# Attention gathers in a graph network: 16 nodes by 8 slots against 32 nodes by 4 slots, with a count of rounds for each group of 32 and new bounds of the kept counts

## The chip, the cores and the metric

The kernel runs on one core of one Trainium2 chip. The metric is the device time of one execution in microseconds (us). A core has five engines, each with its own queue of instructions worked off in order: TensorE (PE) multiplies matrices, VectorE (DVE) and ScalarE (ACT) do elementwise work, GpSimd (POOL) does elementwise work and issues the indirect transfers (gathers and scatters by row index), SyncE (SP) issues plain transfers.

## The reference

Two layers over a graph of 4096 nodes with 128 features. `adj` is a symmetric random matrix with the diagonal set; a node has some 40 to 100 neighbours.

```python
# layer 0: graph attention, 8 heads
Wh = einsum('nd,hde->hne', nodes, W)
f1 = einsum('hnd,hd->hn', Wh, a1);  f2 = einsum('hnd,hd->hn', Wh, a2)
e = leaky_relu(f1[:, :, None] + f2[:, None, :], 0.2)
att = softmax(where(adj > 0, e, -9e15), axis=-1)
h = elu(einsum('hnm,hmd->hnd', att, Wh))
x = elu(concat_heads(h) @ W1 + b1)
x = layernorm(nodes + x) * gamma + beta
# layer 1: every (num_nbr / 2)-th neighbour of a node is dropped, the rest are kept
vals = where(keep[:, :, None], x[None], big)
svals = sort(vals, axis=1)                      # per node and per feature
agg = mean over q in (.25, .5, .75) of svals[ceil(q * n_keep) - 1]
out = (0.5 * agg + 0.5 * x) @ W.T + b + x
```

## The kernel before

The program goes through four stages.

**Lists.** `neighbours` reads `adj` and makes, for every node, the list of its neighbours' ids (up to `C1` = 104). `arrange` counts them, works out how many are kept, and sorts the nodes by that count: 32 tiles of 128 nodes, tile 0 with the smallest counts. Its result goes to `meta_d` in DRAM, one row of `MW` = 216 words for each node at its place in the order. A row is cut into `SL` parts of `PART` words; in each part the first `FULL` words hold every `SL`-th neighbour (padded with row 0 of the table, whose logit is a large negative number), the others hold the kept ids for layer 1 and the node's own id. `column(k)` says where the k-th of these other words stands.

**The choice of a branch.** The tables `LOW` and `HIGH` are the smallest and the largest kept count that tile t is taken to hold. `arrange` compares the graph's counts with them (`lower`, `upper`, lines 367 to 377 and 527) and raises a flag if one is broken. With the flag raised `general` runs, a path without these lists; otherwise `gat` and `sparse` do.

**`gat`, layer 0 on the lists.** For a tile of 128 nodes the lists are gathered so that one indirect transfer fills 128 partitions with `NJ` nodes times `SL` slots: before, 16 nodes by 8 slots. A tile is `GR` = 8 groups of 16 nodes, and a group takes `rounds[t]` transfers, the largest count of the tile plus 2 divided by 8 and rounded up, so that all groups of a tile take the same number. A transfer (line 637) brings for each partition a row of 136 numbers from `xf_d`: 128 features and 8 logits f2. `probabilities` copies the logits out (`f2`, ACT, line 661), turns them through DRAM (`e_d`) so that a partition is one node, does the softmax, and turns the result back (`p_d`, `pr`). `combine` builds for every group the tile `spread` (DVE, line 701): for each round, the probability of partition p at the columns of its node and zero at the columns of the other nodes, `NJ` * `H` = 128 columns. Then one float32 matmul a round (line 711), with the gathered rows as the stationary operand and `spread` as the moving one, adds into `ps_z`. Two products with `W` and `W1`, the layernorm and a scatter of the 128 finished rows to `x1_d` (line 758) follow. The loop issues the gathers of tile t + 1 ahead of the work on tile t. Gathered rows live in a pool of 18 buffers (`nb`), 8 of them a tile. The work on tile t + 1 is told to stand behind the last steps of tile t.

**`sparse`, layer 1.** For tile t all `HIGH[t]` rows of kept neighbours are gathered from `x1_d` (line 1185, one transfer for each place in the list, and one, `xs`, for the nodes' own rows). A network of comparators then sorts the places, elementwise over nodes and features: `compare` copies the low operand (ACT, line 1219), and takes minimum and maximum (DVE, lines 1220 and 1221), or only one of them where only one is needed (lines 1223 and 1225). `places(t)` gives, from `LOW[t]` and `HIGH[t]`, the ranks that a quartile can fall on; only comparators that these need are kept. Where `HIGH[t]` is over 64 and not over 80, the rows past 64 (`extra`) are sorted apart and brought in at the wanted ranks through the tile `cut` (lines 1235 to 1250). `finish` weighs the ranks that can be a quartile (one step at line 1265 or 1268 for each), and ends with a small product, two additions (`o`, lines 1280 and 1281) and a scatter (line 1282). Comparators of the second half of tile t - 1 and of the first half of tile t are interleaved on DVE. `rows` has 3 buffers, so the gathers of tile t + 1 wait for the last step at line 1268 of tile t - 2.

A scheduler puts each engine's instructions in an order when the kernel is built; steps of one tile can stand among those of another. The addition `o` = `xs` + bias (line 1280) of a tile stands early, soon after its gathers begin.

Of the kernel before, what the change touches and what calls it, by code (L numbers as in the profile page):

```python
# [38 lines left out]
F32 = mybir.dt.float32  # L39
F16 = mybir.dt.float16  # L40
BF = mybir.dt.bfloat16
I32 = mybir.dt.int32
# [3 lines left out]
ALU = mybir.AluOpType  # L46
# [4 lines left out]
P = 128  # L51
N = 4096
D = 128
NT = N // P
H = 8
NCH = N // 512
BIG = float(2**53)
# [15 lines left out]
CAND = C1 + C2 + C3 * PEELS  # L73
WBITS = 16
NG1 = N // WBITS
SL = 8
NJ = P // SL
GR = P // NJ
XF = D + 2 * H
FULL = C1 // SL  # L80
PART = FULL + 14
MW = SL * PART
NODE, POS = C1, C1 + 3
MIDDLE = 64
# [261 lines left out]
def arrange(tc, nc, c, lists, spill, negative, meta_d, flag_d):  # L346
# [5 lines left out]
    with tc.tile_pool(name="ar", bufs=1) as tp, tc.tile_pool(  # L352
        name="ar2", bufs=2
# [28 lines left out]
        for t in range(NT):  # L382
# [32 lines left out]
        own = tp.tile(classes, BF, name="own_c")  # L415
# [4 lines left out]
            op=ALU.is_equal,  # L420
# [4 lines left out]
        width = NT // 4 * NC  # L425
# [34 lines left out]
        for i in (1, 2):  # L460
            at = tp.tile([P, NT], F32, name="at", bufs=2)
# [13 lines left out]
        first = tp.tile([P, NT], F32, name="first")  # L475
# [104 lines left out]

def gat(tc, nc, c, xf_d, meta_d, w, w1, b1, gamma, beta, x1_d):

    rounds = [-(-(h + 2) // SL) for h in HIGH]
    most = max(rounds)
    with ExitStack() as ctx:
        one = ctx.enter_context(tc.tile_pool(name="ga1", bufs=1))
        tp = ctx.enter_context(tc.tile_pool(name="ga2", bufs=2))
        rowp = ctx.enter_context(tc.tile_pool(name="ga3", bufs=2 * GR + 2))
        dram = ctx.enter_context(tc.tile_pool(name="ga_d", bufs=2, space=DRAM))
        psum = ctx.enter_context(tc.tile_pool(name="ga_ps", bufs=2, space=PSUM))  # L590
        psum1 = ctx.enter_context(tc.tile_pool(name="ga_ps1", bufs=1, space=PSUM))
# [12 lines left out]
        ids = one.tile([P, GR * sum(rounds)], I32, name="ids")  # L604
        first = [GR * sum(rounds[:t]) for t in range(NT)]
        for t in range(NT):
            r = rounds[t]
            nc.sync.dma_start(
                out=ids[:, first[t] : first[t] + GR * r].rearrange("p (g r) -> p g r", g=GR),
                in_=dram_view(meta_d, t * P * MW, [[PART, P], [PART * P, GR], [1, r]]),  # L610
            )
# [8 lines left out]
        own, f1, den = small[:, :NJ], small[:, NJ : NJ + H], small[:, NJ + H :]  # L620
        nc.vector.reduce_sum(own, c["idf"].rearrange("p (j s) -> p j s", s=SL), axis=AX.X)

        def load(t):
            r = rounds[t]
            me = tp.tile([P, XF], F32, name="me", bufs=3)
            nc.gpsimd.indirect_dma_start(
                out=me,
                out_offset=None,
                in_=xf_d,
                in_offset=bass.IndirectOffsetOnAxis(ap=info[:, t, 1:2], axis=0),  # L630
            )
            groups = []
            for g in range(GR):
                rows = rowp.tile([P, most, D + H], F32, name="nb")
                for i in range(r):
                    at = first[t] + g * r + i
                    nc.gpsimd.indirect_dma_start(  # L637
                        out=rows[:, i, :],
                        out_offset=None,
                        in_=xf_d,  # L640
                        in_offset=bass.IndirectOffsetOnAxis(ap=ids[:, at : at + 1], axis=0),
                    )
                groups.append(rows)
            return me, groups

        def probabilities(t, me, groups):

            r = rounds[t]
            width = r * H
            e_d = dram.tile([P * SL * most * H], F32, name="e_d")  # L650
            p_d = dram.tile([P * SL * most * H], F32, name="p_d")

            def by_row(d):
                return dram_view(d, 0, [[width, P], [width * P, GR], [1, width]])

            def by_node(d):
                return dram_view(d, 0, [[width * SL, P], [1, width * SL]])

            f2 = tp.tile([P, GR, most * H], F32, name="f2")
            for g, rows in enumerate(groups):  # L660
                nc.scalar.copy(  # L661
                    f2[:, g, :width].rearrange("p (r h) -> p r h", h=H), rows[:, :r, D:]
                )
# [24 lines left out]
            nc.sync.dma_start(out=pr[:, :, :width], in_=by_row(p_d))  # L688
            return pr

        def combine(t, me, groups, pr):

            r = rounds[t]
            zT = tp.tile([P, H, P], F32, name="zT", bufs=1)
            for half in range(2):
                ps_z = psum.tile([P, GR // 2, NJ * H], F32, name="ps_z")
                for k in range(GR // 2):
                    g = half * (GR // 2) + k
                    spread = tp.tile([P, most, NJ, H], F32, name="spread")
                    shape = [P, r, NJ, H]  # L700
                    nc.vector.tensor_tensor(  # L701
                        spread[:, :r],
                        pr[:, g, : r * H]
                        .rearrange("p (r h) -> p r h", h=H)
                        .unsqueeze(2)
                        .to_broadcast(shape),
                        own.unsqueeze(1).unsqueeze(3).to_broadcast(shape),
                        op=ALU.mult,
                    )
                    for i in range(r):  # L710
                        nc.tensor.matmul(  # L711
                            ps_z[:, k, :],
                            groups[g][:, i, :D],
                            spread[:, i].rearrange("p j h -> p (j h)"),
                            start=i == 0,
                            stop=i == r - 1,
                        )
# [12 lines left out]
            for h in range(H):  # L730
# [991 lines left out]
```

## Time and profile before

| what | us |
|---|---|
| median of three runs | 9627.47 (9623.37 to 9630.22) |
| the profiled execution | 8855.54 |
| its span, first to last instruction | 8853.8 |
| lists and arrange, to the first gather of `gat` at | 872.77 |
| `gat`, from there to the start of its last scatter | 2998.89 |
| `sparse`, 3874 to 8843 | 4969 |

The profiled execution was 771.9 us shorter than the median of the runs; the profile shows nothing of that difference. Busy time of an engine is the time in which at least one of its instructions ran. An idle time in brackets is that of the engine just before the instruction, with what ended it; `issue` is time in which nothing that the profile shows was waited for.

Over the span the engines were busy: PE 890.4 us, DVE 6064.2 us, ACT 2178.9 us, POOL 4453.2 us.

### The profile page before, as it was taken

The numbers are of one execution on the slowest core, as the hardware profiler recorded it, in microseconds if no ns is written. First come the engines' busy times: TensorE is split into PE (matmuls) and PEld (weight loads), VectorE is DVE, ScalarE is ACT, GpSimd is POOL, SyncE is SP. The second block draws the span as 40 slices with busy tenths as digits, with TensorE's granted clock in tenths as the row PEclk, the third lists the DMA queues.
The fourth block names the chain that finished last, engine by engine and source line by source line (L and its number), as shares of the span: only waits on it lengthen the run. The fifth ranks groups of instructions, "written<-read, shape, count | busy, mean of one in ns | idle before, by whom it ended". The sixth has DMA issues, their size and how long they took to land. (4 is left out here: it accounts for less than half of the span.)

```text
span 8853.8 us, 31211 instructions
## 1 busy us (share of the span) xinstructions
PE 890.4 (10%) x6299; PEld 816.5 (9%) x6299; DVE 6064.2 (68%) x8106; ACT 2178.9 (25%) x2202; POOL 4453.2 (50%) x4633
## 2 busy tenths in 40 slices
PE   2110122122322322210000000000000000000000
PEld 1110122121222222210000000000000000000000
DVE  7996122222222222227989999999999988999999
ACT  2110011010100000003333333333333333333333
POOL 0002777777777777755444544545354543345510
PEclk5555566566666666655555555555555555555555
DMA  3221333333323332321111111111011110011100
GB/s 137 106 89 26 72 67 70 70 66 69 70 67 72 67 68 68 68 48 40 34 31 30 37 30 30 36 28 38 25 38 25 35 30 23 23 30 34 32 7 1
DMA packets 285892, 428.52 MB, mean 48 GB/s; under 512 B 179669, under 2 KB 196440, under 8 KB 277496
## 3 DMA queue, kind: packets, MB, share of 16 engines
q0 software_dynamic: 146240, 309.79, 15.4%
q1 hardware_dynamic: 122886, 109.19, 4.0%
q10 hardware_dynamic: 16562, 7.44, 0.3%
q14 instruction: 151, 1.24, 0.0%
q8 instruction: 53, 0.87, 0.0%
HBM read 397.33 MB, written 28.77 MB: 48 GB/s over the span
## 5 line engine op out<-in xcount | busy, mean ns | idle before, releaser
L1185 POOL DMA_INDIRECT rows<-x_d,info x2114 | 2109.9, 998 | 2310.6 <-DVE agg L1268 1536.5
L637 POOL DMA_INDIRECT nb<-xf_d,ids x2280 | 2159.3, 947 | 699.4 <-issue 661.0
L1219 ACT COPY low<-rows 128x2048 f32<-128x2048 f32 (+8 forms) x1034 | 1588.1, 1552 | 2618.3 <-DVE rows L1221 2305.4
L1220 DVE TENSOR_TENSOR rows<-low,rows 128x2048 f32<-128x2048 f32 (+8 forms) x1034 | 1926.5, 1887 | 195.0 <-ACT low L1219 191.7
L1221 DVE TENSOR_TENSOR rows<-low,rows 128x2048 f32<-128x2048 f32 (+8 forms) x1034 | 1925.0, 1886 | 2.5
L672 DVE TENSOR_TENSOR e<-e,ps_small 128x576 f32<-128x576 f32 (+5 forms) x32 | 23.9, 748 | 1608.6 <-DMA e<-e_d 1608.6
L711 PE MATMUL ps_z<-spread,nb 128*128 128x128 f32 x4560 | 590.1, 298 | 2251.9 <-issue 2115.0
L711 PEld LDWEIGHTS ps_z<-spread,nb 128*128 128x128 f32 x4560 | 584.9, 214 | 2257.0 <-issue 2257.0
L701 DVE TENSOR_TENSOR spread<-pr,ps_small 128x1152 f32<-128x1152 f32 (+5 forms) x256 | 340.6, 1341 | 385.6 <-PE ps_z L711 212.6
L1275 PE MATMUL low<-idf,com 128*128 128x128 f32 x32 | 15.2, 475 | 4913.7 <-DVE rows L1221 3139.5
L1275 PEld LDWEIGHTS low<-idf,com 128*128 128x128 f32 x32 | 5.8, 182 | 4923.1 <-DVE rows L1221 3146.0
L661 ACT COPY f<-nb 128x72 f32<-128x72 f32 (+5 forms) x256 | 64.1, 250 | 1429.2 <-DMA nb<-xf_d,ids 1261.9
L356 POOL IOTA it_s<- 128x104 int32 x1 | 0.2, 215 | 738.7 <-DVE spill L336 738.7
L1219 ACT COPY low_s<-rows 128x512 f32<-128x512 f32 (+3 forms) x361 | 164.3, 476 | 464.7 <-DVE rows L1220 235.1
L1282 POOL DMA_INDIRECT out<-o,info x32 | 38.4, 1200 | 469.4 <-DVE o L1281 463.0
L718 ACT COPY zT<-ps_z 128x512 f32<-128x512 f32 x64 | 37.5, 586 | 863.5 <-PE ps_z L711 863.5
L271 ACT ACTIVATE junk_n<-a_i 128x2048 bf16<-128x2048 int32 x64 | 122.3, 1910 | 470.0 <-DMA a_i<-in_adj 470.0
L1220 DVE TENSOR_TENSOR rows<-low_s,rows 128x512 f32<-128x512 f32 (+3 forms) x361 | 179.0, 506 | 0.7
L1221 DVE TENSOR_TENSOR rows<-low_s,rows 128x512 f32<-128x512 f32 (+3 forms) x361 | 179.2, 506 | 0.4
L160 DVE MAX8 k<-key 128x8 f32<-128x256 f32 x416 | 160.1, 418 | 1.1
L162 DVE MATCH_REPLACE8 key<-k,key 128x256 f32<-128x256 f32 x384 | 155.6, 412 | 0.0
L280 PE MATMUL ps_words<-nz,pows 128*128 128x256 bf16 x512 | 104.0, 388 | 513.2 <-DVE nz L267 513.2
(190 smaller groups left out, 2317.6 us busy)
## 6 DMA issues: line engine op xcount, KB each, us to landing
a_i<-in_adj SPq DMA_DIRECT2D x64, 1024.0 KB, 7.0
nb<-xf_d,ids POOLq DMA_INDIRECT x2280, 2.6
rows<-x_d,info POOLq DMA_INDIRECT x2114, 2.5
e_d<-f SPq DMA_DIRECT2D x12, 288.0 KB, 2.8
e<-e_d SPq DMA_DIRECT2D x12, 288.0 KB, 2.8
p_d<-e SPq DMA_DIRECT2D x12, 288.0 KB, 2.2
pr<-p_d SPq DMA_DIRECT2D x12, 288.0 KB
info<-meta_d SPq DMA_DIRECT2D x32, 108.0 KB, 2.0
```

Source lines behind the costliest of these rows:

```text
L160: nc.vector.max(out=top, in_=work)
L162: nc.vector.match_replace(out=work, in_to_replace=top, in_values=work, imm_value=gone)
L271: nc.scalar.activation(junk, a_i, AF.Relu, scale=-1.0, accum_out=negative[:, 2 * t + i : 2 * t + i + 1],)
L280: nc.tensor.matmul(ps_w, pows[:, b, :], nz[:, ts(b, NG1)], start=b == 0, stop=b == WBITS - 1,)
L637: nc.gpsimd.indirect_dma_start(out=rows[:, i, :], out_offset=None, in_=xf_d, in_offset=bass.IndirectOffsetOnAxis(ap=ids[:, at : at + 1], a ...
L661: nc.scalar.copy(f2[:, g, :width].rearrange("p (r h) -> p r h", h=H), rows[:, :r, D:])
L701: nc.vector.tensor_tensor(spread[:, :r], pr[:, g, : r * H] .rearrange("p (r h) -> p r h", h=H) .unsqueeze(2) .to_broadcast(shape), own.uns ...
L711: nc.tensor.matmul(ps_z[:, k, :], groups[g][:, i, :D], spread[:, i].rearrange("p j h -> p (j h)"), start=i == 0, stop=i == r - 1,)
L1185: nc.gpsimd.indirect_dma_start(out=row, out_offset=None, in_=x1_d, in_offset=bass.IndirectOffsetOnAxis(ap=info[:, col : col + 1], axis=0),)
L1219: nc.scalar.copy(packed, lows)
L1220: nc.vector.tensor_tensor(lows, packed, highs, op=ALU.min)
L1221: nc.vector.tensor_tensor(highs, packed, highs, op=ALU.max)
```

## The change

The gathers of layer 0 take 32 nodes by 4 slots (`SL` 4, so `NJ` 32 and `GR` 4). In place of one count of rounds a tile there is one for each group of 32 nodes, from the new table `GROUP`; `HIGH` is the largest of each row of it, and `LOW` and `HIGH` have other values. The rows of a group no longer stand in one buffer: they come in runs of up to `RUN` = 11 rounds, each with a buffer of its own, in a pool of 22 (each with 11 places of 136 numbers in place of 13). `spread` is built run by run, with 32 * 8 = 256 columns a round. Groups with fewer rounds than the largest of their tile get the rest of `f2` filled with the large negative number. `arrange` checks the upper bounds group by group. `sparse` itself has no changed line; its plans follow from `LOW` and `HIGH`.

```diff
-SL = 8
+SL = 4
+RUN = 11
...
-PART = FULL + 14
+PART = FULL + 112 // SL
...
-LOW = (34, 46, 50, 50, 52, 54, 54, 54, 56, 56, 56, 58, 58, 58, 60, 60,
-       60, 62, 62, 62, 62, 64, 64, 64, 66, 66, 68, 68, 70, 72, 74, 76)
-HIGH = (50, 54, 54, 56, 56, 58, 58, 60, 60, 62, 62, 62, 64, 64, 64, 64,
-        66, 66, 66, 68, 68, 68, 70, 70, 72, 72, 74, 74, 76, 78, 80, 98)
+
+LOW = (28, 48, 50, 52, 54, 54, 56, 56, 58, 58, 58, 60, 60, 60, 62, 62,
+       62, 64, 64, 64, 66, 66, 66, 68, 68, 68, 70, 70, 72, 74, 74, 78)
+GROUP = (
+    (46, 48, 48, 50), (50, 52, 52, 52), (52, 52, 54, 54), (54, 54, 54, 54),
+    (54, 56, 56, 56), (56, 56, 56, 56), (56, 58, 58, 58), (58, 58, 58, 58),
+    (58, 58, 58, 58), (60, 60, 60, 60), (60, 60, 60, 60), (60, 60, 60, 62),
+    (62, 62, 62, 62), (62, 62, 62, 62), (62, 62, 62, 64), (64, 64, 64, 64),
+    (64, 64, 64, 64), (64, 64, 64, 64), (66, 66, 66, 66), (66, 66, 66, 66),
+    (66, 66, 66, 66), (66, 68, 68, 68), (68, 68, 68, 68), (68, 68, 68, 70),
+    (70, 70, 70, 70), (70, 70, 70, 70), (72, 72, 72, 72), (72, 72, 72, 74),
+    (74, 74, 74, 74), (76, 76, 76, 76), (78, 78, 78, 80), (80, 82, 84, 100),
+)
+HIGH = tuple(max(g) for g in GROUP)
...
-            low = [(t + 1) * P for t in range(NT) if HIGH[t] // 2 + 1 == i]
+            low = [
+                t * P + (g + 1) * NJ
+                for t in range(NT)
+                for g in range(GR)
+                if GROUP[t][g] // 2 + 1 == i
+            ]
...
-    rounds = [-(-(h + 2) // SL) for h in HIGH]
-    most = max(rounds)
+    rounds = [[-(-(h + 2) // SL) for h in g] for g in GROUP]
+    most = max(max(r) for r in rounds)
...
-        rowp = ctx.enter_context(tc.tile_pool(name="ga3", bufs=2 * GR + 2))
+        rowp = ctx.enter_context(tc.tile_pool(name="ga3", bufs=22))
...
-            for g in range(GR):
-                rows = rowp.tile([P, most, D + H], F32, name="nb")
-                for i in range(r):
-                    at = first[t] + g * r + i
...
-                groups.append(rows)
+            for g, r in enumerate(rounds[t]):
+                runs = []
+                for k in range(0, r, RUN):
+                    n = min(RUN, r - k)
+                    rows = rowp.tile([P, RUN, D + H], F32, name="nb")
+                    for i in range(n):
+                        at = first[t] + g * max(rounds[t]) + k + i
...
+                    runs.append((k, n, rows))
+                groups.append(runs)
...
-            for g, rows in enumerate(groups):
-                nc.scalar.copy(
-                    f2[:, g, :width].rearrange("p (r h) -> p r h", h=H), rows[:, :r, D:]
-                )
+            for g, runs in enumerate(groups):
+                if rounds[t][g] < r:
+                    nc.vector.memset(f2[:, g, rounds[t][g] * H : width], -BIG)
+                for k, n, rows in runs:
+                    nc.scalar.copy(
+                        f2[:, g, k * H : (k + n) * H].rearrange("p (r h) -> p r h", h=H),
+                        rows[:, :n, D:],
+                    )
...
-                    spread = tp.tile([P, most, NJ, H], F32, name="spread")
...
-                    for i in range(r):
-                        nc.tensor.matmul(
-                            ps_z[:, k, :],
-                            groups[g][:, i, :D],
-                            spread[:, i].rearrange("p j h -> p (j h)"),
-                            start=i == 0,
-                            stop=i == r - 1,
+                    for first_round, n, rows in groups[g]:
+                        spread = tp.tile([P, RUN, NJ, H], F32, name="spread")
...
+                        for i in range(n):
+                            nc.tensor.matmul(
+                                ps_z[:, k, :],
+                                rows[:, i, :D],
+                                spread[:, i].rearrange("p j h -> p (j h)"),
+                                start=first_round + i == 0,
+                                stop=first_round + i == rounds[t][g] - 1,
+                            )
```

More of the change, by code (lines that the diff above doesn't have):

```diff
@@ L603, in gat @@
             nc.sync.dma_start(out=x1_d[row : row + 1, :], in_=pad)
-        ids = one.tile([P, GR * sum(rounds)], I32, name="ids")
-        first = [GR * sum(rounds[:t]) for t in range(NT)]
+        first = [GR * sum(max(r) for r in rounds[:t]) for t in range(NT + 1)]
+        ids = one.tile([P, first[NT]], I32, name="ids")
         for t in range(NT):
-            r = rounds[t]
+            r = max(rounds[t])
             nc.sync.dma_start(
-                out=ids[:, first[t] : first[t] + GR * r].rearrange("p (g r) -> p g r", g=GR),
+                out=ids[:, first[t] : first[t + 1]].rearrange("p (g r) -> p g r", g=GR),
                 in_=dram_view(meta_d, t * P * MW, [[PART, P], [PART * P, GR], [1, r]]),
@@ L623, in load @@
         def load(t):
-            r = rounds[t]
             me = tp.tile([P, XF], F32, name="me", bufs=3)
@@ L632, in load @@
             groups = []
-            for g in range(GR):
-                rows = rowp.tile([P, most, D + H], F32, name="nb")
-                for i in range(r):
-                    at = first[t] + g * r + i
[L637 to L641, printed above, removed]
-                    )
-                groups.append(rows)
+            for g, r in enumerate(rounds[t]):
[5 more added lines that the diff above has]
+                        at = first[t] + g * max(rounds[t]) + k + i
+                        nc.gpsimd.indirect_dma_start(
+                            out=rows[:, i, :],
+                            out_offset=None,
+                            in_=xf_d,
+                            in_offset=bass.IndirectOffsetOnAxis(ap=ids[:, at : at + 1], axis=0),
+                        )
+                    runs.append((k, n, rows))
+                groups.append(runs)
             return me, groups
         def probabilities(t, me, groups):
-            r = rounds[t]
+            r = max(rounds[t])
             width = r * H
@@ L659, in probabilities @@
             f2 = tp.tile([P, GR, most * H], F32, name="f2")
-            for g, rows in enumerate(groups):
-                nc.scalar.copy(
-                    f2[:, g, :width].rearrange("p (r h) -> p r h", h=H), rows[:, :r, D:]
-                )
+            for g, runs in enumerate(groups):
[6 more added lines that the diff above has]
+                    )
             nc.sync.dma_start(out=by_row(e_d), in_=f2[:, :, :width])
@@ L691, in combine @@
         def combine(t, me, groups, pr):
-            r = rounds[t]
             zT = tp.tile([P, H, P], F32, name="zT", bufs=1)
@@ L698, in combine @@
                     g = half * (GR // 2) + k
-                    spread = tp.tile([P, most, NJ, H], F32, name="spread")
[L700 to L709, printed above, removed]
-                    for i in range(r):
-                        nc.tensor.matmul(
-                            ps_z[:, k, :],
-                            groups[g][:, i, :D],
-                            spread[:, i].rearrange("p j h -> p (j h)"),
-                            start=i == 0,
-                            stop=i == r - 1,
-                        )
+                    for first_round, n, rows in groups[g]:
+                        spread = tp.tile([P, RUN, NJ, H], F32, name="spread")
+                        shape = [P, n, NJ, H]
+                        nc.vector.tensor_tensor(
+                            spread[:, :n],
+                            pr[:, g, first_round * H : (first_round + n) * H]
+                            .rearrange("p (r h) -> p r h", h=H)
+                            .unsqueeze(2)
+                            .to_broadcast(shape),
+                            own.unsqueeze(1).unsqueeze(3).to_broadcast(shape),
+                            op=ALU.mult,
+                        )
+                        for i in range(n):
[5 more added lines that the diff above has]
+                                stop=first_round + i == rounds[t][g] - 1,
+                            )
                 nc.scalar.copy(
```

## The prediction

> **What bounds the kernel now.** The page's chain of waits names only the last scatter, so I read the kernel by stages: first the table of slices, then busy time over the two long stages, then the costliest groups, then the timeline where one stage hands over to the next.
>
> ```profile
> DVE  7996122222222222227989999999999988999999
> POOL 0002777777777777755444544545354543345510
> ```
>
> Slices are 221 us. From slice 3 to 17 POOL is the only engine over half busy (`gat`); from slice 18 on DVE is (`sparse`). The windows say the same (after the length: PE, PE's weight load, DVE, ACT, POOL, then clock, DMA share and GB/s):
>
> ```profile
> 832.00:3872.00 3040.00, 721.38 (x5584) 704.03 (x5584) 721.05 (x1155) 282.84 (x607) 2248.62 (x2373) 0.62 0.31 68
> 3874.00:8843.00 4969.00, 41.12 (x97) 22.06 (x97) 4579.25 (x3912) 1752.58 (x1428) 2177.89 (x2178) 0.50 0.12 30
> ```
>
> ```profile
> L1185 POOL DMA_INDIRECT rows<-x_d,info x2114 | 2109.9, 998 | 2310.6 <-DVE agg L1268 1536.5
> L637 POOL DMA_INDIRECT nb<-xf_d,ids x2280 | 2159.3, 947 | 699.4 <-issue 661.0
> L1220 DVE TENSOR_TENSOR rows<-low,rows 128x2048 f32<-128x2048 f32 (+8 forms) x1034 | 1926.5, 1887 | 195.0 <-ACT low L1219 191.7
> L711 PE MATMUL ps_z<-spread,nb 128*128 128x128 f32 x4560 | 590.1, 298 | 2251.9 <-issue 2115.0
> L701 DVE TENSOR_TENSOR spread<-pr,ps_small 128x1152 f32<-128x1152 f32 (+5 forms) x256 | 340.6, 1341 | 385.6 <-PE ps_z L711 212.6
> ```
>
> In `gat` a gather (L637) is 0.947 us and its idle before is 0.30 us of issue, almost nothing else: a gather every 1.25 us, 160 in 200 us, back to back. The stage costs its count of gathers. In `sparse` gathers wait for DVE (L1268, 1536.5 us); they are cover, and DVE's work and its idle 390 us (4969 - 4579) make the time. Its idle has two names: 191.7 us for ACT copies and 181.4 us for `xs`, shown here where they are long:
>
> ```profile
> 7187.02 0.96 POOL L1185 DMA_INDIRECT rows<-x_d,info  x1 [68.59 <-DVE agg L1268]
> 7253.19 0.29 DVE L1280 TENSOR_TENSOR o<-xs,lb 128x128 f32<-128x128 f32 x1 [36.74 <-DMA xs<-x_d,info]
> 7444.98 0.29 DVE L1280 TENSOR_TENSOR o<-xs,lb 128x128 f32<-128x128 f32 x1 [35.05 <-DMA xs<-x_d,info]
> ```
>
> The last tile of `gat` has no cover: POOL waits for its whole chain.
>
> ```profile
> 3833.82 8.38 PE L711 MATMUL ps_z<-spread,nb 128*128 128x128 f32 x48 [104.21 <-issue]
> 3871.66 0.98 POOL L758 DMA_INDIRECT x_d<-s,info  x1 [64.14 <-DVE s L757]
> ```
>
> **What the Trainium skill says.** "DMA: Bandwidth & Descriptors" (SWDGE vs HWDGE vs iDMA) has GpSimd compute the descriptors of its transfers in software; the 0.947 us that POOL is busy with each gather agree, so fewer gathers shorten POOL's queue. "FP8 and Floating Point Precision" (TensorE Precision Notes) gives a true float32 product four passes; the trace has two records a product (4560 for 2280), so two passes a record. "TensorE: Matmul & The Clock Gate" (Back-to-back issue gap) gives a pass N/2.4 + 2.5 ns at full clock and N/1.2 at half: at 128 columns a record is 112 ns, and the last tile's 180 records in 20.26 us are 112.6 ns each, at full clock. "VectorE: DVE Perf Modes" (Mode 1×) gives one result a cycle at 0.96 GHz; 2282 ns for 2048 elements agrees, so a comparator's cost is its elements.
>
> **The change part by part**, against the span of 8853.8 us.
>
> 1. Gathers of `gat`. Before: rounds from `HIGH`, 285 over the tiles, by 8 groups = 2280. After: (count + 2)/4 rounded up, summed over `GROUP` = 2148. Each group costs a gather as before (same 128 rows of 136 numbers). 132 x (0.947 + 0.304) = **-165 us**. Bounds: -150 to -170.
>
> 2. Matmuls of `gat` are 256 columns wide, 4296 records. By the skill's formula an estimate of 2 x (256/2.4 + 2.5) = 218 ns a record; bounds 200 and 427 (half clock). `spread` doubles in elements: 2148 x 256; from 1353 ns at 1152 and 1.89 us at 1664 elements (1.05 ns each + 0.145) its 257 pieces make 614 us, 273 more. Inside the loop both hide behind gathers. Tile 30's chain ran from 3676 (last logits in) to 3734.8, 58.5 us, of which 22.6 us PE; the rest is 36. After, a mean tile has 67 rounds: 36 + 1.6 (a longer first piece) + 134 x 0.218 + 2 cold = 69 us, against 67 x 1.25 + 2.5 = 86 us of gathers: 17 us of room. Nor do buffers stop POOL: a tile takes 8 of 22, so only its last two wait, for the tile two before. If that cover went, each missing us a tile costs 32 us.
>
> 3. The last tile. 90 rounds: PE 180 x 0.218 + 2 = 41 us against 26.2 us (3833.8 to 3860.1), first piece (2816 elements, 3.1 us) 1.2 us later: **+16 us** (+12 to +60 at half clock).
>
> 4. Comparators of `sparse`. From the plans that `LOW` and `HIGH` give and the mean of each shape in the trace: two-sided pairs 1395 -> 1330, 14450 -> 13996 rows of 128: -139 us on DVE; one-sided 489 -> 476 but longer, +10; `cut` steps 213 -> 183, 202 -> 132 us, -70 (less `extra`, fewer ranks); weights 163 -> 118 at 0.346 us, -16; L1254 -1. Sum -216. Neighbouring records overlap (4838 us of durations, 4579 busy, 3912 records: 0.066 us each), and 218 fewer give 14 back: **-202 us**. ACT sheds copies too and stays under half busy. The 36 fewer gathers (2114 -> 2078) give nothing: a load takes some 90 us of the 190 us between a freed buffer and its first use.
>
> 5. Waits for `xs`. The built queues show where it stands. Rule: it lands (gathers ahead + 1) x 1.25 + 2.7 us after the buffer is free, while DVE has the work between L1268 and L1280. Before, 48 gathers stand ahead in tiles 25 and 26 against 30 us of work: 34 us each (trace 36.7, 35.1); over all tiles from 3 on the rule gives 114 us, the trace 107. After, those two are gone and six tiles have 17 or 19 gathers ahead, some 13 us each: 83 by the rule, 78 scaled: **-30 us** (-45 to 0). At the start, `xs` of tile 2 stands behind 102 row gathers, not 104: **-2.5 us**.
>
> 6. DVE's waits for ACT. 4200 to 6200 (tiles without `extra`) idles 152 us, 23 of it `xs`, some 8 us a tile; later tiles about 3. Eighteen narrow tiles in place of sixteen: **+10 us** (0 to +30).
>
> 7. At nothing: `arrange` (a memset of 896 for 448 elements at 0.43 us, five more POOL memsets at 0.04, hidden by L383 beside them); 13 memsets of `f2` and one more logit copy, under the gathers, the last three under tile 31's; 32 `ids` loads of the same number, the first gather needs the first alone.
>
> Sum: -165 + 16 - 202 - 30 - 2.5 + 10 = -373.5, a span of **8480 us**. The runs' median lies 771.9 us over the profiled execution, whose cause I can't see. Kept whole: 9627.5 - 373.5 = 9254; scaled with the rest (8482/8855.5): 9221. I take the middle, **9237 us**.
>
> **Rivals.**
> - *Forecast*: both stages shrink, 9237. Chance 0.75; its own range 9180 to 9300.
> - *Only the gathers pay.* DVE's queue in `sparse` is reordered throughout; if new waits for ACT or `xs` eat its 220 us, 9627 - 149 = 9478. For: 370 us of such waits now. Against: in late windows DVE is 98% busy, and by the queues' order and these durations every load has 56 us or more to spare before its first use. 0.10, with halves of it between 9300 and 9400.
> - *More than counted*: the unseen 772 us belong to gathers, of which 168 of some 4500 go, and waits shrink: 9150. 0.08.
> - *Slower: PE at half clock.* PE idles most of `gat` (mean clock 0.62). If each tile's products ran cold, the chain would be 38 + 134 x 0.427 = 95 us, over the gathers' 86, and `gat` 32 x 95 + 65 = 3105 us, 106 more than now and still less than `sparse` gains. Slower overall from about 0.45 us a record (99 us a tile); at 0.5, 105 us a tile, `gat` is 3425, and 9627 + 426 - 224 = 9829. Against: 112.6 ns now is full clock, and longer streams leave a smaller cold share. 0.03.
> - *Not what it says: a bound is broken*, and `general` runs. Its attention alone has 8 x 8 x 32 x 2 DVE steps on 512 elements at 0.683 us (L947), 2.8 ms, and its quantiles are many times that: over 20 ms. `LOW` is mostly raised and `GROUP` tight, without margin. Against: drawn from the reference's own generator, every kept count of a group lies within its bound (last group: 96 against 100). 0.02.
> - *No change* needs gains and losses to cancel: 0.02.
>
> Range 9160 to 9340. A measurement here tells about 0.2% from no change. Faster: 0.75 + 0.10 + 0.08 = 0.93; same 0.02; slower 0.05.
>
> **What would show it.** Right: 2148 gathers at 0.95 us with 0.30 us of issue; first gather to last scatter 2850 us; PE records about 220 ns apart; POOL's last wait about 80 us; DVE in `sparse` about 4377 us busy, idle near 365; no `xs` wait over 16 us past the start. Wrong: idle before gathers named PE or DVE (item 2), PE records near 430 ns, DVE idle over 450 us, or `sparse` lines of another branch.

## The result and the profile after

| | us |
|---|---|
| before, median of 4 runs | 9625.42 (9614.84 to 9630.22) |
| after, median of 4 runs | 9762.51 (9752.85 to 9769.31) |
| ratio | 1.0143, 95% interval 1.0126 to 1.0161 |
| predicted | 9237 (9160 to 9340) |

The change made the kernel 1.4% slower; 4% faster had been predicted. The profiled execution after took 9756.76 us, like its other runs, while that of before had taken 8855.54 us, 770 us less than its runs. So these two profiles were not of one kind. The slices of the changed kernel, 244 us each:

```profile
DVE  8993122222222222222339889999999899999999
POOL 0005555555445455555444544455444535463430
```

POOL is about half busy in the attention stage; in the profile before it was at 7 tenths. The windows over the two long stages (after the length: PE, PE's weight load, DVE, ACT, POOL, then clock, DMA share, GB/s):

```profile
875.00:4985.00 4110.00, 1324.90 (x5320) 1099.03 (x5320) 978.20 (x1165) 274.74 (x608) 2094.18 (x2212) 0.65 0.20 47
4988.00:9754.00 4766.00, 41.09 (x97) 22.08 (x97) 4381.61 (x3693) 1693.40 (x1363) 2112.55 (x2142) 0.50 0.12 30
```

`sparse` did what was predicted: DVE 4381.61 us busy (predicted 4377). `gat` is 4110 us long, not 2850, though its gathers cost what they did. The costliest groups say where the engines stood (busy, mean ns of one, then idle before and what ended most of it):

```profile
L655 POOL DMA_INDIRECT nb<-xf_d,ids x2148 | 2032.4, 946 | 1594.8 <-issue 1564.1
L724 DVE TENSOR_TENSOR spread<-pr,ps_small 128x2816 f32<-128x2816 f32 (+8 forms) x257 | 604.7, 2381 | 1664.9 <-remote 1079.4
L741 ACT COPY zT<-ps_z 128x512 f32<-128x512 f32 x64 | 37.5, 586 | 2702.9 <-PE ps_z L734 1584.1
L968 DVE TENSOR_SCALAR cat<-ps_h 128x512 f32<-128x512 f32 x64 | 44.2, 691 | 781.2 <-remote 452.4
L734 PE MATMUL ps_z<-spread,nb 128*128 128x256 f32 x4296 | 1136.1, 430 | 2285.3 <-issue 1498.7
```

A gather is still 0.946 us. The idle before gathers is 1594.8 us, of which 0.30 us for each of 2148 is issue, 644 us; some 950 us are new. One tile in the timeline shows them (start, length, engine and line, in brackets the engine's idle before it and what ended it):

```profile
3010.48 0.96 POOL L655 DMA_INDIRECT nb<-xf_d,ids  x1 [28.81 <-issue]
...
3022.55 1.75 DVE L724 TENSOR_TENSOR spread<-pr,ps_small 128x1536 f32<-128x1536 f32 x1 [1.49 <-PE ps_z L734]
3058.37 4.75 DVE L724 TENSOR_TENSOR spread<-pr,ps_small 128x2816 f32<-128x2816 f32 x2 [34.07 <-remote]
3059.08 0.95 POOL L655 DMA_INDIRECT nb<-xf_d,ids  x1 [6.35 <-issue]
...
3078.54 0.69 DVE L968 TENSOR_SCALAR cat<-ps_h 128x512 f32<-128x512 f32 x1 [15.42 <-remote]
...
3093.97 0.69 DVE L968 TENSOR_SCALAR cat<-ps_h 128x512 f32<-128x512 f32 x1 [14.74 <-issue]
...
3106.65 0.29 DVE L756 TENSOR_TENSOR y<-ps_y,b_ga 128x128 f32<-128x128 f32 x1 [10.60 <-remote]
...
3141.19 0.96 POOL L655 DMA_INDIRECT nb<-xf_d,ids  x1 [28.14 <-issue]
```

From 3010.48 to 3141.19 is one tile, 131 us. POOL issues 34 gathers to 3052.7, is out of buffers, goes on at 3059.08 with 34 more to 3101.3, and then, but for the gather of `me` and the scatter of the tile, issues nothing until the first products of the next tile give buffers back at 3141.19. The steps that wait for TensorE soon after the gathers have begun still wait 1.5 to 3.4 us; the later ones wait long, 34.07, 15.42, 14.74 and 10.60 us. Each of these waits began while gathers were being issued; the first and the last ended some 5.5 us after POOL's last gather before a pause. The 34 us wait is for a buffer that products free which stand in the trace from 3021.11 to 3028.7. What comes late is the word of them: the semaphore that TensorE raises for each product was raised at these times (from the trace's semaphore records):

```
... 3024.64 3027.45 3029.59 3033.08 3035.91 3040.81 3046.41 3052.01 3056.21
3058.31 3058.35 3058.39 3058.43 3058.48 3058.52 3058.56 3058.61
```

While gathers run, one arrives every 2 to 6 us. POOL pauses at 3052.7, and from 3058.31 on eight arrive within 0.3 us, 0.04 us apart. A product of 256 columns takes 0.43 us (the distance of the reports while nothing holds them up), so those had been multiplied before, and only their reports were held up. The Trainium skill's "Perfetto Trace Analysis" (Tensor Engine Instruction) says that the end which the profiler gives for a matmul is an estimate from its size, and that the semaphore update is pushed after that, once the result has been written, and has then still to reach the other engines; this trace agrees, with about 30 us between the two.

Such bursts tell the two profiles apart. During the gathers of `gat` 233 reports of the changed kernel on record came less than 0.06 us after the one before; in the first profile of before there is none.

### The profile page after: what moved, and what is told of

Read it like the earlier page. It is cut to its first block, busy times and chain, and to the rows that moved or that the text cites. A ratio compares the mean times of both kernels' runs of the same rounds, so it can differ in the third digit from the quotient of the medians.

```text
span 9755.0 us, 30041 instructions
## 1 busy us (share of the span) xinstructions
PE 1494.1 (15%) x6035; PEld 1212.3 (12%) x6035; DVE 6124.9 (63%) x7902; ACT 2111.7 (22%) x2138; POOL 4260.1 (44%) x4470
## 5 line engine op out<-in xcount | busy, mean ns | idle before, releaser
L1208 POOL DMA_INDIRECT rows<-x_d,info x2078 | 2042.6, 983 | 2135.0 <-DVE agg L1291 1050.6
L655 POOL DMA_INDIRECT nb<-xf_d,ids x2148 | 2032.4, 946 | 1594.8 <-issue 1564.1
L1242 ACT COPY low<-rows 128x2048 f32<-128x2048 f32 (+9 forms) x1009 | 1548.1, 1551 | 2553.7 <-DVE rows L1244 1709.9
L1243 DVE TENSOR_TENSOR rows<-low,rows 128x2048 f32<-128x2048 f32 (+9 forms) x1009 | 1878.1, 1886 | 208.4 <-ACT low L1242 89.5
L1244 DVE TENSOR_TENSOR rows<-low,rows 128x2048 f32<-128x2048 f32 (+9 forms) x1009 | 1876.3, 1884 | 5.2 <-DVE rows L1243 1.4
L724 DVE TENSOR_TENSOR spread<-pr,ps_small 128x2816 f32<-128x2816 f32 (+8 forms) x257 | 604.7, 2381 | 1664.9 <-remote 1079.4
L734 PE MATMUL ps_z<-spread,nb 128*128 128x256 f32 x4296 | 1136.1, 430 | 2285.3 <-issue 1498.7
L734 PEld LDWEIGHTS ps_z<-spread,nb 128*128 128x128 f32 x4296 | 925.3, 219 | 2488.8 <-issue 1517.4
L1298 PE MATMUL low<-idf,com 128*128 128x128 f32 x32 | 15.1, 473 | 4707.4 <-DVE rows L1244 2075.4
L968 DVE TENSOR_SCALAR cat<-ps_h 128x512 f32<-128x512 f32 x64 | 44.2, 691 | 781.2 <-remote 452.4
L1242 ACT COPY low_s<-rows 128x256 f32<-128x256 f32 (+3 forms) x321 | 144.8, 470 | 399.3 <-DVE rows L1243 129.7
L1244 DVE TENSOR_TENSOR rows<-low_s,rows 128x256 f32<-128x256 f32 (+3 forms) x321 | 157.2, 499 | 3.2 <-remote 1.9
L1243 DVE TENSOR_TENSOR rows<-low_s,rows 128x256 f32<-128x256 f32 (+3 forms) x321 | 156.9, 498 | 1.4 <-ACT low_s L1242 0.7
```

The source lines that it names most:

```text
L655: nc.gpsimd.indirect_dma_start(out=rows[:, i, :], out_offset=None, in_=xf_d, in_offset=bass.IndirectOffsetOnAxis(ap=ids[:, at : at + 1], a ...
L724: nc.vector.tensor_tensor(spread[:, :n], pr[:, g, first_round * H : (first_round + n) * H] .rearrange("p (r h) -> p r h", h=H) .unsqueeze( ...
L734: nc.tensor.matmul(ps_z[:, k, :], rows[:, i, :D], spread[:, i].rearrange("p j h -> p (j h)"), start=first_round + i == 0, stop=first_round ...
L968: nc.vector.tensor_scalar(out, v, 0.0, None, op0=ALU.min)
L1208: nc.gpsimd.indirect_dma_start(out=row, out_offset=None, in_=x1_d, in_offset=bass.IndirectOffsetOnAxis(ap=info[:, col : col + 1], axis=0),)
L1242: nc.scalar.copy(packed, lows)
```

## The experiments

The kernel before was timed beside every group of runs, and it had two times. Each result names its group by a letter. A is the first group, on the chip with number 3 in the record: 9620 us. B is two groups on number 15: 9614 and 9633 us. C is two groups on number 9, 8851 us both, and the last group, some 95 minutes after the first and again on number 3: 8853 us. So A and B are one condition and C another, and the chip's number does not decide between them: 3 was met in both. The times on record (9625, 9762) are like those of A and B, and the first profile of before like C; their chip is not recorded. Ratios are to the kernel before, timed beside the run in the same group.

**Where the 772 us are (A).** The kernel before, unchanged.

> The kernel before, unchanged, profiled once more. Theory A (gathers in flight delay what TensorE reports to the other engines, in most executions): the profiled execution takes about 9620 us like the timed ones, the extra 770 us against the first profile lie between the first gather of the attention stage and its last scatter (about 3770 us there instead of 2999), and the sparse stage stays at 4982 us. Rival B (the 772 us are outside that stage, or not in the device's execution at all): the stage stays near 3000 us, or the profiled execution is near 8855 us again while the timed ones stay at 9625.

Measured 9618.23 us, ratio 0.9998 (0.9989 to 1.0006), and a profiled execution of 9606.8 us. Its windows and groups:

```profile
873.00:4614.00 3741.00, 976.97 (x5584) 920.94 (x5584) 716.69 (x1152) 282.70 (x607) 2217.13 (x2344) 0.60 0.25 54
4617.00:9606.00 4989.00, 41.15 (x97) 22.09 (x97) 4579.96 (x3911) 1752.57 (x1428) 2179.92 (x2178) 0.50 0.12 29
```

```profile
L637 POOL DMA_INDIRECT nb<-xf_d,ids x2280 | 2155.3, 945 | 1002.7 <-issue 994.1
L701 DVE TENSOR_TENSOR spread<-pr,ps_small 128x1152 f32<-128x1152 f32 (+5 forms) x256 | 338.5, 1340 | 2118.5 <-remote 1546.5
```

Theory A has the place right: of the 753 us between the two profiles of one kernel, 741 lie in `gat` (3740 against 2999). The mechanism that it names is not shown by this run alone, though 606 reports came less than 0.06 us after the one before here. A tile takes 115 us there, not 91, and the gathers are no longer back to back. It was so before the change too; the first profile could not show it.

The trace also counts reports. The Trainium skill's "DMA: Bandwidth & Descriptors" (Why a DMA increments its semaphore by 16 and not by 1) says that each of the 16 DMA engines of a transfer adds one to the semaphore. The trace agrees: a gather ends in 16 packets of 4 bytes, on A, B and C from about 0.9 us after POOL is done with it. What is recorded of the increments differs, and so does what is recorded of TensorE's reports:

```
gat from 1400 us on        increments recorded per gather   PE reports due   PE reports recorded
before, first profile      16.0                             1906             1903
before, on A               3.9                              1895             1603
after, on record           3.5                              1828             1495
```

**Which part loses (A).** Bounds alone, with 16 nodes by 8 slots:

```diff
-LOW = (34, 46, 50, 50, 52, ...
-HIGH = (50, 54, 54, 56, 56, ...
+LOW = (28, 48, 50, 52, 54, ...
+GROUP = (...)
+HIGH = tuple(max(g) for g in GROUP)
```

> Only the new bounds, with 16 nodes by 8 slots as before: LOW and HIGH of the changed kernel, the attention stage and arrange as in the kernel before (2240 gathers there instead of 2280). Theory A (the loss is the grouping's, the bounds gain as predicted): the sparse stage falls by 212 us as in the changed kernel, the attention stage by 40 x 1.25 = 50 us or a little more, in all 9625 - 262 = 9363 us, 9330 to 9400. Rival B (the new bounds themselves bring the loss): at or above 9625 us.

The grouping alone, with the old bounds:

```diff
 # in the changed kernel
-LOW = (28, 48, ...
+LOW, HIGH = those of before
+GROUP = tuple((h,) * 4 for h in HIGH)
```

> Only the grouping of 32 nodes by 4 slots, with the old bounds: 2208 gathers of the attention stage instead of 2280, the sparse stage as before. Theory A (the grouping brings the loss): the sparse stage at 4980 us and the attention stage about 4180 us, the changed kernel's 4109 us times 2208/2148 less its constant part, so 9625 + 350 = 9975 us, 9850 to 10100. Rival B (the grouping is harmless): 9625 us or less by up to 90 us.

Measured: bounds alone 9344.08 us (0.971, 0.9692 to 0.9728), 2.9% faster than before; the grouping alone 10099.05 us (1.0497, 1.048 to 1.0515). The bounds take 220 us from `sparse` (4993.5 to 4773.7) and 44.5 from `gat`. The grouping leaves `sparse` at 4989 and adds 499 us to `gat`, with 72 gathers fewer. Theory A holds for both, for the grouping at the upper end of its range. With the new bounds in both, the grouping adds 414 us to `gat` (3695.5 to 4109.3).

**More buffers for `spread` (A).**

```diff
-rowp = ctx.enter_context(tc.tile_pool(name="ga3", bufs=22))
+rowp = ctx.enter_context(tc.tile_pool(name="ga3", bufs=18))
-spread = tp.tile([P, RUN, NJ, H], F32, name="spread")
+spread = tp.tile([P, RUN, NJ, H], F32, name="spread", bufs=4)
```

> The changed kernel with four buffers for spread instead of two and 18 for the gathered rows instead of 22. Theory A (TensorE's reports come late while gathers are issued, and each spread that waits for one hands the delay on): with four buffers only four of a tile's eight spreads wait for a product of the same tile, so the chain of a tile loses one or two of its waits of 15 to 34 us and the attention stage 500 to 1500 us: 8300 to 9300 us in all. Rival B (the last results of a tile are late however they are asked for, since the reports form one queue): within 100 us of the changed kernel's 9762. Rival C (fewer buffers for rows make POOL wait, and its pauses are what lets the reports through): in between or better than 9762 without the spreads' waits having gone.

Measured 9728.37 us (1.0112, 1.0095 to 1.013), as rival B had it:

```profile
L968 DVE TENSOR_SCALAR cat<-ps_h 128x512 f32<-128x512 f32 x64 | 44.3, 692 | 1755.5 <-PE ps_h L751 1187.2
L724 DVE TENSOR_TENSOR spread<-pr,ps_small 128x2816 f32<-128x2816 f32 (+8 forms) x257 | 600.1, 2380 | 441.5 <-DMA pr<-p_d 158.8
```

DVE's waits before `spread` fell from 1664.9 to 441.5 us, and those before `cat` came in their place. In a tile the time went into the step before: ACT's last copy of `ps_z` into `zT` starts 51.2 us after the last spread, in place of 12.1 us (means, see the table below). The wait moved to the next result that was asked of TensorE.

**TensorE's time or its number of reports (B).** Half of the columns, or every second product (the `stop` mark, left out here, moves to the last product made):

```diff
 # half columns
+some = NJ // 2 if first_round + i else NJ
-ps_z[:, k, :], ..., spread[:, i]
+ps_z[:, k, : some * H], ..., spread[:, i, :some]
 # half of the products
-for i in range(n):
+for i in range(0, n, 2):
```

> The changed kernel with all of a group's products after the first on half of their columns (the first 16 of 32 nodes): the other half of each attention sum is left out. As many products, about half of TensorE's time on them. Theory A (what counts is the number of results that TensorE reports while gathers are issued, not its time): within 150 us of the changed kernel's 9762. Rival B (TensorE's own time in each tile's chain, which the grouping doubled): 134 records x 0.106 us = 14 us less a tile, 450 us in all, so about 9310 or lower.

> The changed kernel with only every second round's product made, each 256 columns wide: half of the rounds are left out of each attention sum. Gathers and spreads as in the changed kernel. TensorE's time falls as in the run with half columns, and the number of its reports falls by half too. Theory A (number of reports): clearly below the run with half columns; the 45 us a tile that POOL now waits fall to 25 or less, so 9762 - 32 x 20 = 9120 us or lower. Rival B (TensorE's time): the same as the run with half columns, near 9310. Rival C (neither; the last report of a tile is late whatever stands before it): both near 9762.

Measured 9336.31 us (0.9708, 0.9692 to 0.9724) and 9318.79 us (0.9695, 0.9679 to 0.9711). TensorE's busy time on these products fell from 1136.1 us to:

```profile
L735 PE MATMUL ps_z<-spread,nb 128*128 128x128 f32 (+1 forms) x4296 | 760.2, 349 | 2264.6 <-issue 1672.1
L734 PE MATMUL ps_z<-spread,nb 128*128 128x256 f32 x2340 | 712.8, 472 | 1527.1 <-issue 1080.6
```

Theory A was wrong here, and rival B right, with 9310: TensorE's time counts, and the number of its reports hardly. `gat` is 3704 us with half columns, 405 us less than in the changed kernel, and 8 more than with the bounds alone on A (3695.5). So the added width of the products is about the whole of the 414 us that the grouping costs. What else the grouping changes, 92 gathers fewer and spreads of twice the size, comes to nothing together; no run takes these two apart in this condition.

**Air between gathers (B).** A clearing of a scratch tile on POOL after each gather, 256 or 1024 elements wide:

```diff
+nc.gpsimd.memset(pace, 0.0)
```

> The changed kernel with one small clearing of a scratch tile (128x256) on POOL after each gather, about 0.35 us: a gather every 1.6 us instead of 1.25. Theory A (gathers issued back to back hold up the reports of the other engines, and a little air lets them through): tiles at 67 x 1.6 + 3 = 110 us instead of 128, the stage 3600 us instead of 4109, 9250 us in all, TensorE's reports regular during the gathers. Rival B (the air doesn't help, gathers hold up reports at this rate too, and each tile costs its gathers plus the same 45 us of waiting): 67 x 0.35 x 32 = 750 us more, 10500 us. Rival C (the chain of a tile takes its 128 us whatever POOL does): unchanged, 9762 within 50 us.

> The same with a scratch tile of 128x1024, about 1.1 us: a gather every 2.35 us. Theory A: reports regular, POOL never waits, the stage 2148 x 2.35 + 150 = 5200 us, 10850 us in all. Rival B (gathers plus 45 us of waiting a tile): 4109 + 2148 x 1.1 = 6470 us, 12100 us in all. Rival C (a chain of 128 us a tile): as theory A in time, since 67 x 2.35 = 157 us is over it, but the reports stay irregular.

The short one took 9698.06 us (1.0087, 1.007 to 1.0104) and tests nothing: the scheduler had put 1801 of the 2148 clearings into blocks of 50 and more when the kernel was built (POOL's queue in the program stands in the same order as the trace), and the gathers still followed each other in 1.25 us (median). In the long one each clearing stands between two gathers. It took 10298.08 us (1.0711, 1.069 to 1.0732); there is a gather every 2.09 us, and:

```profile
L657 POOL DMA_INDIRECT nb<-xf_d,ids x2148 | 2049.9, 954 | 361.7 <-issue 355.1
L727 DVE TENSOR_TENSOR spread<-pr,ps_small 128x2816 f32<-128x2816 f32 (+8 forms) x257 | 602.9, 2381 | 597.3 <-PE ps_z L737 428.7
L744 ACT COPY zT<-ps_z 128x512 f32<-128x512 f32 x64 | 37.5, 586 | 1442.5 <-PE ps_z L737 1442.5
L971 DVE TENSOR_SCALAR cat<-ps_h 128x512 f32<-128x512 f32 x64 | 44.3, 692 | 256.8 <-PE ps_h L754 216.9
```

DVE waits 597.3 us before `spread` in place of 1664.9, and 256.8 before `cat` in place of 781.2; 15.1 of 16 increments a gather are recorded, and no report comes less than 0.06 us after the one before; with half columns, in the same group of runs, 391 do. In the same condition, and with the same products, nothing is held up once gathers are 2.09 us apart. That is theory A's mechanism; its time of 10850 was too high, since the interval came to 2.09 and not 2.35 us.

**The softmax out of the chain, and more gathers (C, then B).** In `combine`, what the next tile's softmax must stand behind:

```diff
-behind = [nc.scalar.sqrt(q, var).ins]
-behind.append(nc.vector.tensor_add(s, s, bc["beta"]).ins)
+behind = [last_spread.ins, last_copy.ins]
```

and in `load` of the changed kernel, one gather more after each run, into a spare buffer:

```diff
+nc.gpsimd.indirect_dma_start(out=spare, out_offset=None, in_=xf_d,
+    in_offset=bass.IndirectOffsetOnAxis(ap=ids[:, at : at + 1], axis=0))
```

> The changed kernel with one more gather after each run of rows (its last one again, into a spare buffer that nobody reads): 257 more gathers, eight a tile. Theory A (the attention stage is set by the chain of each tile, and POOL waits for it 45 us a tile): most of the 10 us a tile lies in that wait; 9762 + 0 to 120 us. Rival B (the stage costs its count of gathers, as the prediction had it, 1.25 us each): + 321 us, 10083 us.

> The run with the new bounds alone (16 nodes by 8 slots, 9344 us), and in addition the softmax of tile t + 1 told to stand behind the last spread and the last copy of ps_z of tile t, and no longer behind its last steps; the whole work is the same. Theory A (the chain of a tile sets the stage, 113.7 us, of which 20.2 us lie between the end of one tile and the first spread of the next): most of the 20 us goes, until the gathers with 70.6 x 1.25 + 2.5 = 91 us a tile take over: 12 to 20 us x 31, so 8720 to 8970 us. Rival B (gathers set the stage): 9344 within 50 us. Rival C (the time of a tile is its gathers plus what has to follow them, so that what leaves the chain comes back as a longer wait for TensorE's results): 9250 to 9344 us.

> The same on the changed kernel: the softmax of tile t + 1 behind the last spread and the last copy of ps_z of tile t. Theory A (chain): 20 us of the 129 us a tile go, and with 109 us the chain is still over the gathers' 86: 31 x 20 = 620 us, so 9140 us, 9050 to 9300. Rival B (gathers set the stage): 9762 within 50 us. Rival C (what leaves the chain comes back as a longer wait for TensorE's results): 9600 to 9762 us.

They met condition C, where the kernel before took 8851.49 us: 8805.09, 8581.42 and 8480.71 us. None of the expectations had that condition in mind. So the changed kernel itself was needed there:

> The changed kernel, unchanged. Theory A (two conditions of the chip; where TensorE's results are not held up by gathers, the stage costs its gathers, as predicted): if the kernel before takes about 8851 us here, this one takes 8851 - 373 = 8478 us, 8450 to 8510, below the run with 257 more gathers (8805) by their 321 us; if it takes about 9620, this one takes 9762 again. Rival B (the changed kernel is slower in both conditions): above 8851 or above 9620.

It met C again: before 8850.72 us, the changed kernel **8478.31 us** (8478.01 to 8480.39), ratio 0.9579 (0.9562 to 0.9596). Three runs beside it (e13, e14, e15) and two later ones (e17, e18, on number 3) also met C and repeated the three times above to within 2 us. On C, 257 more gathers cost 327 us (1.27 us each), the earlier softmax nothing (8480.71 against 8478.31): gathers set the stage there. The profile of the changed kernel on C:

```profile
873.00:3720.00 2847.00, 1170.78 (x5320) 985.30 (x5320) 977.68 (x1165) 274.79 (x608) 2092.76 (x2212) 0.72 0.30 67
3723.00:8478.00 4755.00, 41.10 (x97) 22.07 (x97) 4381.15 (x3693) 1693.42 (x1363) 2116.49 (x2142) 0.50 0.12 30
```

```profile
L655 POOL DMA_INDIRECT nb<-xf_d,ids x2148 | 2031.1, 946 | 658.3 <-issue 623.3
L724 DVE TENSOR_TENSOR spread<-pr,ps_small 128x2816 f32<-128x2816 f32 (+8 forms) x257 | 603.0, 2381 | 595.8 <-PE ps_z L734 425.5
L741 ACT COPY zT<-ps_z 128x512 f32<-128x512 f32 x64 | 37.5, 586 | 1442.6 <-PE ps_z L734 1442.6
```

Beside the same three groups of the profile on record: the work is equal within 2 us, and the waits are not, 658.3 us against 1594.8 before gathers and 595.8 against 1664.9 before `spread`. No report comes less than 0.06 us after the one before.

The earlier softmax in the changed kernel, tried again, met B:

> The changed kernel with the softmax of the next tile behind the last spread and copy of ps_z. Where the kernel before takes about 9620 us: theory A (the chain of a tile sets the stage) 9050 to 9300 us; rival B (gathers) 9762 within 50; rival C (what leaves the chain comes back as a longer wait for TensorE's results) 9600 to 9762. Where it takes about 8851: 8480 us, which tells nothing new.

Measured 9509.73 us, ratio 0.9871 (0.9851 to 0.9891). That lies between theory A and rival C. The parts of a tile, as means over tiles 4 to 27, worked out from the starts in the traces: from the end of the tile before to the first `spread`, the spreads, then to the last `zT` copy, the last `cat` and `y`, and to the last step of `s`. Where gathers set the stage, the first part holds the wait for them.

```
us                          tile   to 1st   spreads  to zT   to cat  to y   to end
before, first profile        91.3   60.2     17.1     2.6     2.7    3.4    5.2
before, on A                114.8   20.4     72.0     8.8     4.3    4.2    5.1
after, on record            129.2   20.6     64.5    12.1    15.3   11.5    5.2
more buffers, on A          128.4   27.0     23.9    51.2     8.8    12.2    5.2
half columns, on B          114.2   19.2     61.7    19.1     4.6    4.5    5.1
long pace, on B             142.0   92.4     31.6     5.9     2.7    3.4    6.0
earlier softmax, on B       120.6    3.0     64.4    12.0    26.7    6.0    8.6
after, on C                  86.5   34.7     31.4     5.9     2.7    3.4    8.2
```

With the earlier softmax the first spread follows the tile before in 3.0 us and not 20.6, but the step from `zT` to `cat` grew from 15.3 to 26.7: half of the gain came back as a longer wait. It gives 1.3% over the kernel before on B, and 4.2% on C. What a gather costs in the condition of A and B was to be shown by the run with more gathers. It met C both times that it was tried again, the last time with this expectation, and took 8806.03 us:

> The changed kernel with 257 more gathers, eight a tile. Where the kernel before takes about 9620 us: theory A (the chain sets the stage and POOL's gathers lie in its shadow) 9762 + 0 to 120 us; rival C (the waits for TensorE's results in the chain end only when POOL pauses, so that gathers and chain add up) 9762 + 240 to 330 us, near 10080. Where it takes about 8851: 8805 us, which tells nothing new.

## Why the prediction was wrong

The sum was right for the profile that it was made from, and its transfer to the runs was not. Point by point, on C (span 8853.8 to 8478.6, -375.2; predicted -373.5 and 8480):

- Items 1 and 3, gathers and the last tile: `gat` fell by 153.4 us (2998.9 to 2845.5), predicted 165 - 16 = 149. POOL's last wait was 76.89 us, predicted about 80.
- Item 2, the wider products and spreads hidden under the gathers: held on C; 34 records of a run took 7.61 us, 224 ns each against 218.
- Items 4 to 6, `sparse`: -223.0 us, predicted -224.5. DVE 4381 us busy (4377). Its `xs` waits were 145.4 us, 36 less; predicted 30. Past the start there are six, 11.9 to 13.0 us each, and the two of 35 us are gone, as the queues' order had said.
- Item 7: the lists' stage is 874.0 us, 1.2 more.

In the runs, `sparse` fell by the same 222.9 us (4993.5 on A to 4770.6). `gat` rose by 369 (3740.0 to 4109.3). Two steps failed there. The first is the transfer, "The runs' median lies 771.9 us over the profiled execution, whose cause I can't see. Kept whole: 9627.5 - 373.5 = 9254": the 772 us are no constant beside the sum; 741 of them were waits in the very stage that the change works on. The second follows from it, in item 2: "Inside the loop both hide behind gathers". The room exists on C: 86.5 us a tile against a chain of 70.5 from the last copy of the logits to the end of the tile (predicted 86 and 69). In the runs' condition that chain takes 126.9 us, and what is held up is some 60 us a tile: from the first spread to the end a tile of the changed kernel takes 108.6 us, against 50 with the long pace; that of before 94.4 us, against 31 in the first profile. So before the change the chain was already the longer of the two, 115 us a tile to 91, and what the wider products add comes through whole, 405 us for the stage.

The rival "More than counted: the unseen 772 us belong to gathers" had their stage right and drew the wrong sign, since they are waits for TensorE and fall with no gather. "PE at half clock" gave the nearest time, 9829 us, by naming the chain that outlasts the gathers; its mechanism did not occur, as runs of products went at 224 ns a record in the profile on record too (34 in 7.61 us), and TensorE was busy with them only 97 us longer than on C (1136.1 against 1039.5), 3 us a tile. The 430 ns of the L734 line are the mean duration of one record, not the distance to the next; on C they are 405. That this rival came near was luck.

The range failed for the same reason. A difference of 8% between profile and runs was over four times its whole width of 180 us, and no case asked what each item is worth if it sits in `gat`: 24 us a tile, more than the 17 us of room.

What stays open is why TensorE's reports are held up in one condition and not in the other, what carries them, whether the recording of an execution has a part in it (fewer increments are recorded there), and the price of a gather in that condition. Nothing in these traces tells.

## What to carry to other kernels

Where the profiled execution and the timed runs differ, find out in which stage before carrying a sum from one to the other: profile the kernel once more, or ask of each item what it is worth if that stage has another bound. A trade of gathers for longer TensorE work pays only where the gathers are the bound. And where a kernel has two times, a change is compared in both conditions, and the condition is read from the kernel before timed beside it, not from the chip's number: this change is 1.4% slower in one and 4.2% faster in the other, while the bounds alone gained 2.9% on A, and the changed kernel with the earlier softmax 1.3% on B and 4.2% on C.

## What the runs showed of the hardware

- One kernel, two times: 9605 to 9647 us on A and B, 8848 to 8855 us on C, over all timed runs of the kernel before. The chip with number 3 showed both, some 95 minutes apart.
- On A and B, with gathers issued every 1.25 us, TensorE's reports came late, in the tile shown by about 30 us (products to 3028.7, their last report at 3058.61), and then in a burst 0.04 us apart; at one gather in 2.09 us there was no such delay and no burst (reports less than 0.06 us apart: 233 in the changed kernel on record, none with the long pace or on C). DVE and ACT handed on to each other in the same stretches without such delays (`cat` on DVE to 3079.23, on ACT from 3079.27).
- There, 3 to 4 increments of 16 a gather are in the record, in place of 15 to 16, though the 4-byte packets that carry them left on time.
